# Attention weights exponentiated key by key without subtracting the row maximum, and normalised after the value matmul

## The chip, the cores and the metric

One core of one Trainium2 chip. The metric is the device time of one execution in microseconds (us); less is better. Of the kernel before there are two unprofiled runs, 6692.37 and 6696.81 us (median 6694.59), and one profiled execution.

## What is computed

The reference is one layer on x of shape [2, 256, 128, 128] (batch, time, band, channel), all in float32. Three residual steps follow one another:

```python
xt = _ln(x, ln_t_w, ln_t_b).transpose(0, 2, 1, 3)
x = x + _mha(xt, t_wi, t_bi, t_wo, t_bo, H_T, cm).transpose(0, 2, 1, 3)
xf = _ln(x, ln_f_w, ln_f_b)
x = x + _mha(xf, f_wi, f_bi, f_wo, f_bo, H_F, bm)
xn = _ln(x, ln_n_w, ln_n_b)
h = jax.nn.gelu(xn @ w1.T + b1, approximate=False)
x = x + (h @ w2.T + b2)
```

`_mha` is attention with 4 heads of 32 channels: scores q.k / sqrt(32) plus a mask, softmax over the keys, the weighted sum of the values, and an output matrix. The first runs over the 256 times of each band under a causal mask (`cm`), the second over the 128 bands of each time under a mask that lets through keys at most 16 bands away (`bm`). The feed-forward widens 128 channels to 512. Matrices are normal numbers times 0.02, biases are zero, norm weights are one.

## The kernel before

The work is done in groups of four token tiles (`NT`) of 128 tokens by 128 channels.

**The time stage** has 128 groups of two bands each. `xt` is loaded for eight bands at once on SP's queue (L278), POOL adds the output bias into `rd` (L282), `attention` runs, and `rd` goes to a DRAM tensor `x1` (L287).

**The band stage** has 32 blocks of 16 time steps. A block loads `xb` (L299), adds the bias on POOL (L301), runs `attention` on four groups one after the other, and then the feed-forward on the same four (L310 to L332): `hp` (w1, L316), gelu on ACT (L317), `zp` (w2, L327), the sum on DVE (L331), and the store.

**Inside a group.** `norm_transposed` takes means and variances on DVE (L118, L119), the inverse deviation on POOL (L121, L122) and the normed tokens `xh` on DVE (L126), and transposes them on PE into `xp`. ACT moves `xp` to SBUF with the norm's weight and bias (`xnT`, L131). From there PE makes `qp`, `kp` and `vp` (L144, L148, L153); ACT writes `qT` and `kT` (L146, L150), DVE writes `v` (L157). A score bank `sp` holds two heads, with queries on the partitions and keys along the row. The mask is put in first by a bfloat16 matmul of the identity with a mask tile (L166), then come the score matmuls over the 32 channels of a head (L173). DVE takes the negated row maximum `nmax` (L181 for bands, L187 for time), ACT exponentiates with it as the bias and adds up each row (L195, one instruction per head and query tile, with its accumulator read). DVE takes the reciprocal (L203), POOL multiplies the weights (L206 or L214), PE transposes each 128x128 block of weights (`tp`, L221), DVE and ACT bring them back to SBUF as `pT` (L226, L228), and PE multiplies them with the values (`op`, L239). ACT copies `op` out (`oT`, L245), PE applies the output matrix (`yp`, L248), DVE adds it to the residual (L249).

The order of each engine's queue is set when the program is built, by the tile framework's scheduler. `ps` has four banks of PSUM for everything but the scores, `ps_s` two tiles of two banks. A manual dependency (L255) makes exponentials and gelus take turns by the block, since they need different ACT tables.

## Time and profile before

| | us |
|---|---|
| median of the two runs | 6694.59 |
| span of the profiled execution, first to last instruction | 6687.7 |
| time stage, first to last `yp` on t_wo | 43.0 to 3075.2 |
| band stage, first to last `yp` on f_wo | 3095.0 to 6651.6 |
| PE busy | 4965.1 (74%) |
| ACT busy | 3223.4 (48%) |
| DVE busy | 2769.3 (41%) |
| POOL busy | 2263.4 (34%) |
| mean granted TensorE clock | 0.840 |

The profiled execution has no time of its own beside its span; the median of the runs is 6.9 us above that span. The shares are means over two stages. In the views of the trace a row gives the engine, the source line, the operation, what it writes `<-` what it reads, the shapes and a count. In the timeline a row begins with its start and its length in us, and ends with the idle time before it and what ended that. PEld is the loading of weights into the array, which overlaps the matmuls. A float32 matmul stands in the trace as two passes, so four matmuls of 128 columns are counted as x8. In the table of windows the column PEclk is the granted TensorE clock, 1.00 or 0.50 at any moment.

### The profile page before, as it was taken

To read this page: it belongs to the slowest core of one execution; us is meant where nothing else is said; L and a number is where in the kernel's file an instruction comes from. 1 tells how busy PE (TensorE), PEld (TensorE's weight loads), DVE (VectorE), ACT (ScalarE), POOL (GpSimd) and SP (SyncE) were. 2 spreads that over 40 slices of the span, in tenths; PEclk is the share of its full clock that TensorE was granted. 3 is DMA by queue.
4 is the path that set the end of the run, shared out by engine and by line. 5 is a ranking of instruction groups with operands and counts; after the bars stand their busy time and mean duration, and the time that the engine had idled before them with its cause. 6 is when DMAs were issued, how large, how long until landed. Compare 5 with 4: busy or idle time off the path is not lost. (4 is left out here: it accounts for less than half of the span.)

```text
span 6687.7 us, 95401 instructions
## 1 busy us (share of the span) xinstructions
PE 4965.1 (74%) x34688; PEld 3392.3 (51%) x34816; DVE 2769.3 (41%) x8068; ACT 3223.4 (48%) x10688; POOL 2263.4 (34%) x2348
## 2 busy tenths in 40 slices
PE   6777777777777777777777777777676767677767
PEld 4444454444444444454555555555454545455555
DVE  4444444444444444434344444444344444444433
ACT  4444444444444444444454444444444444454544
POOL 4333333333333333433232323233333333233332
PEclk8878787778787877788888888888888888888888
DMA  1000000000000000000000000000000000000000
GB/s 48 20 24 25 23 20 24 24 23 20 24 24 23 20 24 23 24 20 20 24 15 24 14 26 14 26 13 26 13 26 13 26 13 26 13 26 13 20 7 13
DMA packets 222968, 141.61 MB, mean 21 GB/s; under 512 B 7968, under 2 KB 205984, under 8 KB 222496
## 3 DMA queue, kind: packets, MB, share of 16 engines
q1 hardware_dynamic: 221248, 134.45, 7.1%
q8 instruction: 274, 4.49, 0.3%
q14 instruction: 198, 1.62, 0.1%
q10 hardware_dynamic: 1248, 1.05, 0.1%
HBM read 68.36 MB, written 67.11 MB: 20 GB/s over the span
## 5 line engine op out<-in xcount | busy, mean ns | idle before, releaser
L195 ACT ACTIVATE p<-sp,nmax 128x128 f32<-128x128 f32 (+1 forms) x4096 | 1547.6, 414 | 870.0 <-DVE nmax L187 553.6
L221 PE MATMUL tp<-ident,p 128*128 128x128 f32 x5120 | 1207.6, 401 | 275.6 <-POOL p L206 228.0
L221 PEld LDWEIGHTS tp<-ident,p 128*128 128x128 f32 x5120 | 930.1, 209 | 743.0 <-POOL p L206 394.6
L214 POOL TENSOR_TENSOR p<-p,rsum 128x256 f32<-128x256 f32 (+1 forms) x1024 | 823.9, 826 | 952.2 <-DVE rsum L203 820.9
L206 POOL TENSOR_TENSOR p<-p,rsum 128x1024 f32<-128x1024 f32 x256 | 485.2, 1895 | 1493.5 <-DVE rsum L203 1493.5
L195 ACT ACTIVATION_READ_ACCUMULATOR p<-sp,nmax 128x1 f32 x4096 | 929.0, 227 | 0.0
L228 ACT COPY pT<-tp 128x384 f32<-128x384 f32 (+1 forms) x768 | 395.1, 518 | 945.8 <-PE tp L221 942.5
L226 DVE COPY pT<-tp 128x384 f32<-128x384 f32 (+1 forms) x768 | 453.8, 598 | 698.9 <-PE tp L221 689.3
L173 PE MATMUL sp<-kT,qT 32*128 32x128 f32 (+1 forms) x8192 | 740.7, 362 | 0.0
L166 PEld LDWEIGHTS <-ident_b 128*128 128x128 bf16 x1536 | 193.8, 128 | 1007.0 <-issue 663.8
L166 PE MATMUL sp<-mask_t,ident_b 128*128 128x384 bf16 x1024 | 383.1, 472 | 384.6 <-ACT p L195 381.7
L203 DVE RECIPROCAL rsum<-rsum 128x4 f32<-128x4 f32 (+1 forms) x768 | 141.9, 185 | 1221.9 <-ACT p L195 1204.0
L239 PE MATMUL op<-pT,v 128*32 128x128 f32 (+1 forms) x8192 | 526.6, 319 | 86.6 <-DVE pT L226 55.0
L166 PE MATMUL sp<-mask_f,ident_b 128*128 128x512 bf16 x384 | 204.3, 601 | 517.0 <-ACT p L195 517.0
L173 PEld LDWEIGHTS sp<-kT,qT 32*128 32x128 f32 x8192 | 490.8, 214 | 172.9 <-issue 142.1
L317 ACT ACTIVATE hT<-hp,cols_sb 128x512 f32<-128x512 f32 x512 | 351.8, 687 | 392.3 <-PE hp L316 389.5
L187 DVE TENSOR_REDUCE nmax<-sp 128x2 f32<-128x256 f32 (+1 forms) x1024 | 505.0, 545 | 56.6 <-PE sp L173 56.5
L131 ACT ACTIVATE xnT<-xp,cols_sb 128x512 f32<-128x512 f32 x384 | 298.4, 777 | 475.0 <-PE xp L129 475.0
L327 PEld LDWEIGHTS zp<-w2T_sb,hT 128*128 128x128 f32 x4096 | 487.5, 192 | 61.5 <-issue 58.4
L316 PE MATMUL hp<-xnT,w1T_sb 128*128 128x512 f32 x1024 | 471.9, 599 | 42.8 <-ACT xnT L131 27.8
L327 PE MATMUL zp<-w2T_sb,hT 128*128 128x128 f32 x4096 | 499.0, 275 | 0.1
L121 POOL TENSOR_SCALAR rstd<-mv 128x4 f32<-128x4 f32 x384 | 91.8, 242 | 1190.5 <-DVE mv L119 1190.5
(55 smaller groups left out, 5974.5 us busy)
## 6 DMA issues: line engine op xcount, KB each, us to landing
xt<-in_x SPq DMA_DIRECT2D x64, 512.0 KB, 5.5
x<-rd SPq DMA_DIRECT2D x256, 128.0 KB, 1.9
out<-res SPq DMA_DIRECT2D x128, 256.0 KB, 2.3
xb<-x SPq DMA_DIRECT2D x32, 0.5 KB, 6.2
w1T_sb<-in_w1T ACTq DMA_DIRECT2D x1, 256.0 KB, 5.4
w2T_sb<-in_w2T ACTq DMA_DIRECT2D x1, 256.0 KB, 7.1
t_wiT_sb<-in_t_wiT ACTq DMA_DIRECT2D x1, 192.0 KB, 2.5
f_wiT_sb<-in_f_wiT ACTq DMA_DIRECT2D x1, 192.0 KB, 4.5
```

What stands on the lines that cost most here:

```text
L166: nc.tensor.matmul(sp[:, j, 0 : nb * P], ident_b, mask.rearrange("p a b -> p (a b)"), start=True, stop=False,)
L173: nc.tensor.matmul(sp[:, j, n * P : (n + len(ks)) * P], qT[r, qi * P : (qi + 1) * P], kT[r, ks[0] * P : (ks[-1] + 1) * P], start=False, st ...
L187: nc.vector.tensor_reduce(nmax[:, :, ri : ri + 1], sp[:, :, n * P : (n + len(ks)) * P], AX.X, ALU.max, negate=True,)
L195: e = nc.scalar.activation(p[:, j, n * P : (n + len(ks)) * P], sp[:, j, n * P : (n + len(ks)) * P], AF.Exp, bias=nmax[:, j, ri : ri + 1], ...
L206: nc.gpsimd.tensor_tensor(pv, pv, rsum.rearrange("p j n -> p (j n)").unsqueeze(2).to_broadcast([P, 2 * nb, P]), ALU.mult,)
L214: nc.gpsimd.tensor_tensor(pv, pv, rsum[:, :, ri : ri + 1].to_broadcast([P, 2, len(ks) * P]), ALU.mult,)
L221: nc.tensor.transpose(tp[:, n * P : (n + 1) * P], p[:, j, n * P : (n + 1) * P], ident)
L226: nc.vector.tensor_copy(t, tp[:, 0 : nb * P])
L228: nc.scalar.copy(t, tp[:, 0 : nb * P])
L239: nc.tensor.matmul(op[r, qi * P : (qi + m) * P], v[:, ki, r], pT[bi, h][:, n * P : (n + m) * P], start=first, stop=last,)
L316: nc.tensor.matmul(hp_, w1T_sb[:, j * P : (j + 1) * P], xnT, start=True, stop=True)
L327: nc.tensor.matmul(zp[:, i], hT[:, j, i * P : (i + 1) * P], w2T_sb[:, j, :], start=(j == 0), stop=(j == NI - 1),)
```

## The change

- `fold` (new, runs once at the start) multiplies the norm's weights and the scale into copies of the projection matrices (`wf`, `w1f`), carries the norm's biases into `bq` and into the row that is added to the residual, and negates the output matrices (`wn`). It bounds the scores by the Gram matrices of the folded query and key weights and leaves a flag, which every engine loads into a register.
- If the flag is set, `bounded_path` runs, otherwise `shifted_path`, which is the code of before. Both are in the program. The bound is a property of the weights. For these weights the sum that is tested is about 128 times 0.0016 times 0.051, that is 0.0105, and the limit is 900/(128 x 129), that is 0.0545, so the flag is set.
- In `bounded_path` a score bank holds one head with the keys on the partitions and the queries along the row. There is no mask matmul, no maximum, no bias of the exponential and no accumulator. One exponential covers 384 columns (time, L539) or 512 (bands, L582).
- Masked weights are set to 0 afterwards, in SBUF, by POOL's affine_select: four of 512 elements per partition per time group (L542), two of 2048 per band group (L584).
- The weights are already in the layout that the value matmul reads, so the transposes `tp` and the copies `pT` are gone, and so are the reciprocal and POOL's multiplication.
- A matmul of the weights with a matrix of ones gives the sum over keys, repeated over a head's 32 channels (`rp`, L561 and L565, or L596). `finish` takes the inverse on ACT as exp(-ln(rp)), sharpens it with a Newton step and scales `op` on DVE (t, u, oT, L508 to L512), and then comes `yp` with the negated matrix.
- `xnT` is a plain copy on ACT; `kT` is a copy on DVE instead of an ACT instruction.
- PSUM is one ring of eight banks.
- A table set that has both exp and ln is loaded ahead of each run of exponentials (L630).
- Groups are still written one after the other.

```diff
--- before.py
+++ after.py
...
+def fold(tc, k):
...
+            wf = const.tile([P, 3 * C], F32, name=f"wf{a}")
+            nc.vector.tensor_scalar(wf[:, 0:C], wi[:, 0:C], col(c0), scale, ALU.mult, ALU.mult)
+            nc.vector.tensor_scalar(wf[:, C : 3 * C], wi[:, C : 3 * C], col(c0), None, ALU.mult)
+            wn = const.tile([P, C], F32, name=f"wn{a}")
+            nc.vector.tensor_scalar(wn, wo, -1.0, None, ALU.mult)
...
+            for h in range(H):
+                r = slice(h * D, (h + 1) * D)
+                nc.vector.tensor_reduce(tests[r, 3 * a : 3 * a + 1], gs[r, r], AX.X, ALU.add)
...
+        tp = pp.tile([P, 6], F32, name="tp")
+        nc.tensor.matmul(tp, k.ones, tests, start=True, stop=True)
+        ok = fp.tile([P, 6], F32, name="ok")
+        for a in range(2):
+            nc.vector.tensor_scalar(
+                ok[:, 3 * a : 3 * a + 1], tp[:, 3 * a : 3 * a + 1], SAFE * SAFE / (C * (C + 1)), None, ALU.is_le
+            )
+            nc.vector.tensor_scalar(
+                ok[:, 3 * a + 1 : 3 * a + 3], tp[:, 3 * a + 1 : 3 * a + 3], LARGE, None, ALU.is_le
...
+        allok = fp.tile([P, 1], F32, name="allok")
+        nc.vector.tensor_reduce(allok, ok, AX.X, ALU.min)
+        flag = const.tile([P, 1], I32, name="flag")
+        nc.vector.tensor_copy(flag, allok)
+    return nc.values_load(flag[0:1, 0:1], min_val=0, max_val=1)
...
+            xnT = work.tile([P, NT * P], F32, name="xnT")
+            nc.scalar.copy(xnT, xp)
+            return xnT
...
+            qp = bank([P, NT * P], "qp")
+            nc.tensor.matmul(qp, wf[:, 0:C], xnT, start=True, stop=True)
+            qT = work.tile([P, NT * P], F32, name="qT")
+            nc.scalar.activation(qT, qp, AF.Identity, bias=k.bq[a], scale=1.0)
...
+            nc.tensor.matmul(kp, wf[:, C : 2 * C], xnT, start=True, stop=True)
+            kT = work.tile([P, NT * P], F32, name="kT")
+            nc.vector.tensor_copy(kT, kp)
...
+            v = work.tile([P, NT, C], F32, name="v")
+            nc.vector.tensor_copy(v, vp)
+            return qT, kT, v
...
+        def exp(p, sp, first):
+            e = nc.scalar.activation(p, sp, AF.Exp)
+            after(e, first)
+            last_exp[0] = e.ins
...
+        def finish(op, rp, dst, a, first):
...
+            ln = work.tile([P, NT * P], F32, name="ln")
+            e = nc.scalar.activation(ln, rp, AF.Ln)
+            after(e, first)
+            r0 = work.tile([P, NT * P], F32, name="r0")
+            exp_ins = nc.scalar.activation(r0, ln, AF.Exp, scale=-1.0)
+            after(exp_ins, first)
+            last_exp[0] = exp_ins.ins
+            t = work.tile([P, NT * P], F32, name="t")
+            nc.vector.tensor_tensor(t, rp, r0, ALU.mult)
+            u = work.tile([P, NT * P], F32, name="u")
+            nc.vector.tensor_tensor(u, op, r0, ALU.mult)
+            oT = work.tile([P, NT * P], F32, name="oT")
+            nc.vector.scalar_tensor_tensor(oT, t, 2.0, u, ALU.subtract, ALU.mult)
+            yp = bank([P, NT, C], "yp")
+            for i in range(NT):
+                nc.tensor.matmul(yp[:, i], oT[:, i * P : (i + 1) * P], k.wn[a], start=True, stop=True)
+            nc.vector.tensor_tensor(dst, yp, dst, ALU.add)
...
+        def over_time(src, dst, first):
...
+            xnT = norm_transposed(src)
+            qT, kT, v = project(xnT, 0)
+            W = 3 * P
+            p = work.tile([P, S, H, W], F32, name="pt", bufs=2)
+            for s in range(S):
+                a = 2 * s * P
+                for h in range(H):
+                    r = rows_of(h)
+                    sp = bank([P, W], "sp")
+                    nc.tensor.matmul(
+                        sp[:, 0 : 2 * P], kT[r, a : a + P], qT[r, a : a + 2 * P], start=True, stop=True
+                    )
+                    nc.tensor.matmul(
+                        sp[:, 2 * P : W], kT[r, a + P : a + 2 * P], qT[r, a + P : a + 2 * P],
+                        start=True, stop=True,
+                    )
+                    exp(p[:, s, h, :], sp, first)
+                for n in (0, 2):
+                    blk = p[:, s, :, n * P : (n + 1) * P]
+                    nc.gpsimd.affine_select(
+                        out=blk, in_=blk, compare_op=ALU.is_ge, fill=0.0, base=0,
+                        pattern=[[0, H], [1, P]], channel_multiplier=-1,
+                    )
+            op = bank([P, S, 2 * P], "op")
+            for s in range(S):
+                for h in range(H):
+                    r = rows_of(h)
+                    nc.tensor.matmul(
+                        op[r, s, :], v[:, 2 * s, r], p[:, s, h, 0 : 2 * P], start=True, stop=False
+                    )
+                for h in range(H):
+                    r = rows_of(h)
+                    nc.tensor.matmul(
+                        op[r, s, P : 2 * P], v[:, 2 * s + 1, r], p[:, s, h, 2 * P : W],
+                        start=False, stop=True,
+                    )
+            rp = bank([P, S, 2 * P], "rp")
+            for h in range(H):
+                nc.tensor.matmul(
+                    rp[rows_of(h), :, :], k.ones[:, 0:D], p[:, :, h, 0 : 2 * P], start=True, stop=False
+                )
+            for h in range(H):
+                nc.tensor.matmul(
+                    rp[rows_of(h), :, P : 2 * P], k.ones[:, 0:D], p[:, :, h, 2 * P : W],
+                    start=False, stop=True,
+                )
+            finish(op.rearrange("p s q -> p (s q)"), rp.rearrange("p s q -> p (s q)"), dst, 0, first)
...
+        def over_bands(src, dst, first):
...
+            xnT = norm_transposed(src)
+            qT, kT, v = project(xnT, 1)
+            p = work.tile([P, H, NT, P], F32, name="pf", bufs=2)
+            for h in range(H):
+                r = rows_of(h)
+                sp = bank([P, NT * P], "sp")
+                for i in range(NT):
+                    c = slice(i * P, (i + 1) * P)
+                    nc.tensor.matmul(sp[:, c], kT[r, c], qT[r, c], start=True, stop=True)
+                exp(p[:, h].rearrange("p i q -> p (i q)"), sp, first)
+            for s in (1, -1):
+                nc.gpsimd.affine_select(
+                    out=p, in_=p, compare_op=ALU.is_ge, fill=0.0, base=BAND,
+                    pattern=[[0, H], [0, NT], [-s, P]], channel_multiplier=s,
+                )
+            op = bank([P, NT * P], "op")
+            for i in range(NT):
+                c = slice(i * P, (i + 1) * P)
+                for h in range(H):
+                    r = rows_of(h)
+                    nc.tensor.matmul(op[r, c], v[:, i, r], p[:, h, i, :], start=True, stop=True)
+            rp = bank([P, NT * P], "rp")
+            for h in range(H):
+                nc.tensor.matmul(
+                    rp[rows_of(h), :], k.ones[:, 0:D], p[:, h].rearrange("p i q -> p (i q)"),
+                    start=True, stop=True,
+                )
+            finish(op, rp, dst, 1, first)
...
+        def exp_tables():
+            e = nc.scalar.preload_act_table_set(EXP_SET)
+            after(e, last_gelu[0])
+            return e.ins
+        first = exp_tables()
...
+    k = load_constants(ctx, tc, x, t_wiT, t_woT, f_wiT, f_woT, w1T, w2T, cols, rows)
+    bounded = fold(tc, k)
+    with tc.If(bounded > 0) as cmp:
+        bounded_path(tc, k, x, out)
+    with cmp.Else():
+        shifted_path(tc, k, x, out)
```

The feed-forward is as before, with `w1f` and the folded bias `b1`. The names below are those of the tables above; a number behind a name is a buffer's.

What PE issues at a border between two time groups, before (the last of a group's transposes and masks, the value matmuls, the output matrix, and the next group's transposes of its tokens):

```order
L221 MATMUL tp<-ident,p 128x128 x6
L166 LDWEIGHTS ident_b
L166 MATMUL sp<-mask_t,ident_b 128x384
...
L221 MATMUL tp<-ident,p 128x128 x2
L239 MATMUL op<-pT,v 32x256 x4
L239 MATMUL op<-pT,v 32x128 x4
...
L248 MATMUL yp<-t_woT_sb,oT 128x128 x4
L129 MATMUL xp<-ident,xh 128x128 x4
L144 MATMUL qp<-xnT,t_wiT_sb 128x512
```

and with the change:

```order
L535 MATMUL sp<-qT,kT 128x128
L550 MATMUL op<-pt,v 32x256 x4
L555 MATMUL op<-pt,v 32x128 x4
...
L561 MATMUL rp<-pt,ones 32x512 x4
...
L565 MATMUL rp<-pt,ones 32x2x128 x4
L515 MATMUL yp<-wn_106,oT 128x128 x4
L466 MATMUL xp<-ident,xh 128x128 x4
L474 MATMUL qp<-xnT,wf_103 128x512
```

Between the scores and `op` stand no matmuls any more, and between `rp` and `yp` none either. The next group's first matmul, `xp`, stands behind `yp` as before.

The same for a band group, before:

```order
L173 MATMUL sp<-kT,qT 128x128 x16
L166 LDWEIGHTS ident_b
L166 MATMUL sp<-mask_f,ident_b 128x512
...
L221 MATMUL tp<-ident,p 128x128 x8
...
L239 MATMUL op<-pT,v 32x128 x16
L248 MATMUL yp<-f_woT_sb,oT 128x128 x4
```

and with the change:

```order
L484 MATMUL vp<-wf_143,xnT 128x128 x4
L581 MATMUL sp<-qT,kT 128x128 x16
L593 MATMUL op<-pf,v 32x128 x16
L596 MATMUL rp<-pf,ones 32x512 x4
L515 MATMUL yp<-wn_146,oT 128x128 x4
```

The two runs of eight transposes that stood between scores and values are gone, and a run of four matmuls of 512 columns is new.

What DVE issues at a border between two band groups, before (the residual of one group, the statistics and normed tokens that its feed-forward will need, and the next group's values):

```order
L249 TENSOR_TENSOR x_26550<-yp,x_26550 128x512
L118 BN_STATS stats<-x_26550 128x6 x4
L119 BN_AGGR mv<-stats 128x2 x4
L126 TENSOR_SCALAR xh<-x_26550,mv,rstd 128x128 x4
L157 COPY v<-vp 128x512
```

and with the change:

```order
L516 TENSOR_TENSOR x_16068<-yp,x_16068 128x512
L455 BN_STATS stats<-x_16068 128x6 x4
L456 BN_AGGR mv<-stats 128x2 x4
L463 TENSOR_SCALAR xh<-x_16068,mv,rstd 128x128 x4
L481 COPY kT<-kp 128x512
L488 COPY v<-vp 128x512
```

The copy `kT`, which the scores wait for, now stands behind `xh`, and `xh` waits for POOL's rstd.

686 lines of the change are left out of this document (433 added, 253 removed).

## The prediction, as it was made before the result

> **What bounds the kernel now.** I read the page first, then the groups of instructions, the timeline of one group of each stage, and last the windows with the granted clock.
>
> ```profile
> span 6687.7 us, 95401 instructions
> PE 4965.1 (74%) x34688; PEld 3392.3 (51%) x34816; DVE 2769.3 (41%) x8068; ACT 3223.4 (48%) x10688; POOL 2263.4 (34%) x2348
> ```
>
> No engine is full, so a chain of waits sets the time. A time group from one `yp` to the next:
>
> ```profile
> 2002.77 1.16 PE L248 MATMUL yp<-t_woT_sb,oT 128*128 128x128 f32 x8 [0.78 <-ACT oT L245]
> 2003.76 0.60 PE L129 MATMUL xp<-ident,xh 128*128 128x128 f32 x4
> 2004.40 0.78 ACT L131 ACTIVATE xnT<-xp,cols_sb 128x512 f32<-128x512 f32 x1 [1.69 <-PE xp L129]
> 2005.23 1.12 PE L144 MATMUL qp<-xnT,t_wiT_sb 128*128 128x512 f32 x2 [0.87 <-ACT xnT L131]
> 2008.03 0.95 PE L173 MATMUL sp<-kT,qT 32*128 32x128 f32 x16
> 2010.50 0.47 ACT L195 ACTIVATE p<-sp,nmax 128x256 f32<-128x256 f32 x1
> 2010.95 0.36 ACT L195 ACTIVATE p<-sp,nmax 128x128 f32<-128x128 f32 x1
> 2012.28 3.22 POOL L214 TENSOR_TENSOR p<-p,rsum 128x256 f32<-128x256 f32 x4 [3.52 <-DVE rsum L203]
> 2024.37 1.03 PE L239 MATMUL op<-pT,v 128*32 128x256 f32 x12 [0.43 <-DVE pT L226]
> 2025.43 0.69 ACT L245 ACTIVATE oT<-op,cols_sb 128x512 f32<-128x512 f32 x1 [0.93 <-PE op L239]
> 2026.17 1.16 PE L248 MATMUL yp<-t_woT_sb,oT 128*128 128x128 f32 x8 [0.78 <-ACT oT L245]
> ```
>
> The next group's `xp` is issued only behind `yp`, so the period of 23.40 us (2002.77 to 2026.17) is the length of the chain. `yp` to scores takes 5.26, scores to `yp` 18.1. A band group, and the feed-forward of a block:
>
> ```profile
> 4017.92 1.16 PE L248 MATMUL yp<-f_woT_sb,oT 128*128 128x128 f32 x8 [0.78 <-ACT oT L245]
> 4023.19 1.72 PE L173 MATMUL sp<-kT,qT 32*128 32x128 f32 x32
> 4025.71 0.37 ACT L195 ACTIVATE p<-sp,nmax 128x128 f32<-128x128 f32 x1 [2.62 <-DVE nmax L181]
> 4036.43 1.06 PE L239 MATMUL op<-pT,v 128*32 128x128 f32 x26 [0.38 <-ACT pT L228]
> 4038.27 1.16 PE L248 MATMUL yp<-f_woT_sb,oT 128*128 128x128 f32 x8 [0.78 <-ACT oT L245]
> 4058.62 1.16 PE L248 MATMUL yp<-f_woT_sb,oT 128*128 128x128 f32 x8 [0.78 <-ACT oT L245]
> 4091.61 1.02 PE L144 MATMUL qp<-xnT,f_wiT_sb 128*128 128x512 f32 x2
> ```
>
> The period is 20.35 us; the last `yp` of a block to the next block's `qp` takes 33.0. The stages end here:
>
> ```profile
> L248 PE MATMUL yp<-t_woT_sb,oT x1024: 275/275/377, 43.0 to 3075.2; 128*128 128x128 f32 x171
> L248 PE MATMUL yp<-f_woT_sb,oT x1024: 275/275/582, 3095.0 to 6651.6; 128*128 128x128 f32 x171
> ```
>
> A time group takes (3075.2 - 43.0)/127 = 23.9 us on the mean, a block of bands (6687.7 - 3079)/32 = 112.8.
>
> The last thing to read is PE's clock (the column behind POOL's).
>
> ```profile
> 43.00:3075.00 3032.00, 2341.70 (x15245) 1497.72 (x15247) 1279.34 (x3762) 1437.18 (x5080) 1136.09 (x1387) 0.80 0.08 23
> 3079.00:6687.70 3608.70, 2600.47 (x19315) 1880.73 (x19441) 1464.08 (x4176) 1771.89 (x5565) 1101.99 (x918) 0.87 0.06 19
> 2004.64:2008.05 3.41, 2.82 (x14) 1.75 (x14) 1.41 (x9) 1.91 (x3) 1.79 (x3) 1.00 0.26 77
> 2008.05:2011.47 3.42, 0.93 (x17) 0.63 (x17) 2.64 (x5) 1.33 (x7) 0.71 (x1) 1.00 0.00 0
> 2014.88:2018.29 3.41, 3.41 (x17) 2.17 (x15) 1.47 (x4) 1.75 (x9) 1.30 (x3) 0.50 0.00 0
> 2018.29:2021.71 3.42, 3.42 (x16) 2.87 (x15) 1.84 (x5) 2.74 (x11) 1.83 (x3) 0.50 0.00 0
> 2021.71:2025.12 3.41, 2.98 (x38) 1.72 (x38) 0.56 (x1) 0.65 (x2) 0.71 (x1) 1.00 0.00 0
> 4004.85:4008.27 3.42, 0.00 (x0) 0.10 (x1) 1.67 (x2) 2.79 (x17) 0.00 (x0) 1.00 0.00 0
> 4008.27:4011.68 3.41, 1.55 (x6) 1.08 (x7) 0.41 (x2) 2.90 (x18) 2.02 (x2) 0.50 0.00 0
> ```
>
> The clock changes at steps of 3.41 us. It halves after a step in which PE did little (0.93 busy, or nothing) and comes back after a step that was full (2018.29). Step 2014.88 was full too and brought nothing; half of its work is `sp`, which uses 32 of 128 rows, so I count such passes at a quarter. Every stretch of PE work below therefore has two prices.
>
> **The change part by part.** The other rows that carry prices:
>
> ```profile
> L228 ACT COPY pT<-tp 128x512 f32<-128x512 f32 x256 | 149.8, 585 | 468.2 <-PE tp L221 468.2
> L249 DVE TENSOR_TENSOR x<-yp,x 128x512 f32<-128x512 f32 x128 | 88.5, 691 | 482.3 <-PE yp L248 482.3
> L97 POOL TENSOR_SCALAR_AFFINE_SELECT mask_f<-mask_f 128x512 bf16<-128x512 bf16 x2 | 1.3, 634 | 0.1
> masks.py:199 POOL TENSOR_SCALAR_AFFINE_SELECT ident<-ident 128x128 f32<-128x128 f32 x1 | 0.3, 292 | 0.0
> L301 POOL TENSOR_TENSOR x<-xb,rows_sb 128x2048 f32<-128x2048 f32 x32 | 145.6, 4550 | 4.8 <-DMA xb<-x 2.4
> ```
>
> *A time group at the full clock.* (a) `yp` to `qp`: 2.46 now, 2.27 with the copy at 585 ns. (b) `qp` to scores 2.80, unchanged: DVE's copy of `kT` (0.69) replaces ACT's 0.69. (c) The first head's scores are two passes of 384 columns at 0.11 us per 128, 0.66, and 0.2 until the reader starts: 0.86. Before, nmax stood here and the first exponential started 2.1 after `sp`. (d) Eight exponentials of 384 columns instead of sixteen with accumulator reads. An ACTIVATE of 256 columns and its read repeat after 0.45 (2010.50 to 2010.95), so I take 0.47 for 384 without a read: 3.8 with the tail. (e) The mask: the row of 128 float32 elements has the same 292 ns as bfloat16, and 634 - 292 for 384 more gives 0.89 ns each, so 512 cost 0.63. The first half's two selects run under the later exponentials; of the second half's, one lies on the path, 0.83 with handovers. (f) `op` of the second half and `rp`. Matmuls of 32 columns run four at a time (26 passes of 128 in 1.06), so 0.11 buys four: 2 x 384 columns of `op` and 2 x 768 of `rp` for each of four heads, 1.94. (g) ln 0.69, exp 0.69 (the `oT` row), t 0.62 and u 0.69 (L249), oT 0.65, with 0.5 of handovers: 3.8. Sum 16.3.
>
> Removed from the path: nmax, reciprocal, POOL's products, 24 transposes, the copies `pT`, eight mask matmuls. DVE's stats, POOL's rstd and `rd`, and SP's stores are issued at the same places and lie under the exponentials as before.
>
> *The same at the half clock.* `yp` and `xp` cost 1.34 more, the projections 2.6, the first scores 0.66, (f) 1.94: 22.8.
>
> *Which of the two.* During (g) PE has nothing to do for 3.8 us, longer than a step, so the clock has halved when `yp` starts. At that clock `yp` and `xp` take 2.7, then comes a gap of 0.8, then 5.2 of projections and the scores. The first step that is at least three quarters full ends between 6 and 10 us after `yp`, about 8, when the projections are nearly through: 1.34 + (8 - 3.5)/2 = 3.6 lost. Then the clock lasts, since the selects' pause is broken by the first half's `op`. I take 16.3 + 3.3 = 19.6 us (3.3, because (f) sometimes and the projections not always pay), 4.3 less than 23.9: 128 x 4.3 = 550 us gained, bounds 140 (22.8) and 970 (16.3).
>
> *A band group at the full clock.* (a) 2.27; (b) 2.80, where `xh` now stands ahead of `kT` on DVE and waits for POOL's rstd, which costs up to 1.5 when the projections are fast and nothing when they are slow; (c) eight passes of 128 on the first head, 0.89 + 0.2; (d) four exponentials of 512, 0.57 apart, 2.4; (e) two selects of 2048 elements, 292 + 1920 x 0.89 = 2.0 each. They cover all heads, so both follow the last exponential, and `op` is queued behind them: 4.15. (f) `op` 0.88 and `rp` 0.86; (g) 3.8. Sum 18.2. Here PE is idle for 5 to 6 us ahead of (f), so (f) runs at the half clock, +1.75; its 3.5 us are too short to bring the clock back; then (g) halves again, and the start of the group loses 3.6 as above. Sum 23.6, against 20.35 before. The first group of a block starts at the full clock behind the feed-forward, `qp` to `yp` 17.8. The feed-forward starts at the half clock now: 33.0 + 1.3 + about 2.1 = 36.4. Block: 17.8 + 3 x 23.6 + 36.4 = 125.0, with two waits for stores and table loads left where they were. That is 12.2 more than 112.8: 32 x 12.2 = 390 us lost. Bounds: -150 (full clock, 108) and +530 (129.5).
>
> *`fold` and the branch*: some twenty short steps of PE and DVE with a handover each, and the loads of x start behind them; 10 to 50 us, I take 25. The program holds both paths, but the one not taken isn't executed.
>
> Sum: 6687.7 - 550 + 390 + 25 = 6553. My terms leave out semaphore waits of a few tens of ns at some forty places of a group, for which I add 0.15 us per group, 40: 6593 for the span. The median of the runs is 6.9 above the span: **6600 us**.
>
> **Rivals.**
>
> *The clock falls only after a step without any PE work.* Then a time group's pause of 3.8 us would hit a whole step of 3.41 one time in nine and the group stay near 16.8, and band groups near 22: 128 x 16.8 + 32 x (17.0 + 3 x 22 + 35) + 60 = 5990 us. The row at 2008.05 speaks against it: 0.93 busy, and half the clock behind it. The Trainium skill ("TensorE: Matmul & The Clock Gate", Part 1) describes it so: half rate is the default, a busy window of 3.4 us releases it and an idle one brings it back; this trace has the length of the window and the two rates, but falls after partly busy ones. By that rule the result would be faster.
>
> *Time groups catch the clock earlier* than 8 us after `yp`, because steps lock to the groups' period: 17.5 to 18.5 per group, 6320 to 6450 us. For it: the bound on the left, 16.3, has PE idle ahead of `op` for under 3 us. Against: the pause (g) is longer than a step in every group.
>
> *Slower: the selects run at POOL's two-operand rate.* 4550 ns for 2048 (L301) instead of 2.0 adds 5.1 per band group and 0.64 per time group: 6600 + 650 + 80 = 7330 us. It decides from about 3.0 us per select of 2048 (6600 + 256 x 1.0 = 6860). Against it: the one float32 row stands at 292.
>
> *Slower: the half clock throughout*, since 32-row score matmuls don't bring it back: 128 x 22.8 + 32 x 129.5 + 80 = 7140 us. For it: 2014.88. Against it: the projections alone hold more than a step.
>
> *The flag is not set* and the old code runs: 6720 us.
>
> **How the numbers follow.** Forecast (6450 to 6800) 0.50; earlier clock 0.17; falls only when idle 0.07; slow selects 0.08; the half clock for longer than forecast, up to throughout (6800 to 7140), 0.16; flag 0.02. A measurement here can tell about 2% from no change, that is 6561 and 6828. Of the forecast 0.17 lies below 6561, so faster 0.17 + 0.17 + 0.07 = 0.41; same 0.33, the flag's 0.02 and 0.02 of the half clock = 0.37; slower 0.14 + 0.08 = 0.22. The range leaves out the fall-only-when-idle case below, and above the slow selects and 0.05 of the half clock: 6290 to 7000.
>
> **What would show it.** Right: `yp` to `yp` near 19.6 in the time stage and 23.6 in the band stage, the time stage shorter by 550 and the band stage longer by 390; PEclk at most 0.80 in both, 0.50 around every band `op`; selects at 0.63 and 2.0 us; no `tp`. Wrong: band groups under 20 us, selects above 3 us, or PEclk near 1.00 in the time stage.

## The result, and the profile after

The changed kernel takes 6321.72 us (two runs, 6314.48 and 6328.95) against 6694.59: ratio 0.9441, 95% interval 0.9423 to 0.9459, 5.6% faster. The forecast was 6600, 1.4% faster. The profiled execution has a span of 6327.0 us.

The page's head, as shown of before:

```profile
span 6327.0 us, 77114 instructions
PE 4254.3 (67%) x31270; PEld 2916.5 (46%) x31270; DVE 2110.8 (33%) x6318; ACT 1834.1 (29%) x3264; POOL 1777.9 (28%) x1830
```

All engines have less to do, and still none is full. The stages, cut at the last `yp` of the time stage (the clock is the column behind POOL's):

```profile
51.10:2386.00 2334.90, 1472.59 (x13221) 968.24 (x13222) 799.10 (x2243) 720.81 (x1525) 628.19 (x879) 0.84 0.11 30
2386.00:6327.00 3941.00, 2758.81 (x17916) 1933.43 (x17914) 1283.46 (x3920) 1106.34 (x1726) 1130.73 (x918) 0.71 0.06 17
```

The time stage went from 3032 to 2335 us. The band stage went from 3609 to 3941, although PE, VectorE and ScalarE issue fewer instructions there (PE 17916 for 19315) and VectorE and ScalarE are busy for less. PE is busy for longer with fewer matmuls, 2759 us for 2600, at a mean clock of 0.71 for 0.87; POOL's 1131 us stand for 1102. A time group in the timeline:

```profile
2000.14 2.05 PE L515 MATMUL yp<-wn,oT 128*128 128x128 f32 x8 [3.52 <-DVE oT L512]
2001.98 1.06 PE L466 MATMUL xp<-ident,xh 128*128 128x128 f32 x4
2003.71 1.12 PE L474 MATMUL qp<-xnT,wf 128*128 128x512 f32 x2 [0.68 <-ACT xnT L468]
2006.57 0.74 PE L532 MATMUL sp<-qT,kT 32*128 32x256 f32 x8
2007.56 3.17 ACT L492 ACTIVATE pt<-sp 128x384 f32<-128x384 f32 x8 [1.99 <-PE sp L535]
2011.48 0.64 PE L550 MATMUL op<-pt,v 128*32 128x256 f32 x8 [0.50 <-POOL pt L542]
2013.75 0.60 ACT L500 ACTIVATE ln<-rp 128x512 f32<-128x512 f32 x1 [3.02 <-PE rp L565]
2017.20 2.05 PE L515 MATMUL yp<-wn,oT 128*128 128x128 f32 x8 [3.57 <-DVE oT L512]
```

17.06 us from `yp` to `yp`, where 19.6 was forecast. `yp` (2.05) runs at half clock, `qp` (1.12) at full clock again. The clock's steps of the same stretch:

```profile
1999.82:2003.24 3.42, 2.90 (x12) 2.53 (x12) 1.03 (x3) 0.17 (x1) 0.00 (x0) 0.50 0.00 0
2003.24:2006.65 3.41, 2.94 (x16) 1.83 (x16) 2.05 (x10) 1.11 (x2) 1.41 (x2) 1.00 0.27 77
2006.65:2010.06 3.41, 1.74 (x36) 1.55 (x40) 0.67 (x1) 2.50 (x7) 1.86 (x4) 1.00 0.00 0
2010.06:2013.48 3.42, 2.92 (x48) 1.10 (x48) 0.00 (x0) 0.67 (x2) 1.67 (x3) 1.00 0.00 0
2013.48:2016.89 3.41, 0.15 (x4) 0.00 (x0) 1.81 (x3) 1.23 (x2) 0.00 (x0) 1.00 0.00 0
2016.89:2020.30 3.41, 2.90 (x12) 2.53 (x12) 1.02 (x3) 0.16 (x1) 0.00 (x0) 0.50 0.02 5
```

`yp` and `xp` together are busy for 2.90 us of one step of 3.42 at half clock, and the clock is back right behind it. A band group:

```profile
4025.74 2.08 PE L515 MATMUL yp<-wn,oT 128*128 128x128 f32 x8 [3.43 <-DVE oT L512]
4029.34 2.08 PE L474 MATMUL qp<-xnT,wf 128*128 128x512 f32 x2 [0.68 <-ACT xnT L468]
4034.50 2.82 PE L581 MATMUL sp<-qT,kT 32*128 32x128 f32 x32
4035.75 2.20 ACT L492 ACTIVATE pf<-sp 128x512 f32<-128x512 f32 x4 [3.61 <-PE sp L581]
4038.03 4.09 POOL L584 TENSOR_SCALAR_AFFINE_SELECT pf<-pf 128x2048 f32<-128x2048 f32 x2 [6.82 <-ACT pf L492]
4042.17 1.94 PE L593 MATMUL op<-pf,v 128*32 128x128 f32 x32 [4.85 <-POOL pf L584]
4045.88 0.60 ACT L500 ACTIVATE ln<-rp 128x512 f32<-128x512 f32 x1 [7.93 <-PE rp L596]
4049.24 2.08 PE L515 MATMUL yp<-wn,oT 128*128 128x128 f32 x8 [3.43 <-DVE oT L512]
```

23.50 us, as forecast (23.6): PE waits 4.85 for the selects, and `op` and the next `yp` and `qp` run at half clock. Here `yp` straddles two steps:

```profile
4023.93:4027.34 3.41, 1.60 (x7) 1.61 (x8) 1.72 (x3) 0.00 (x0) 0.00 (x0) 0.50 0.00 0
4027.34:4030.75 3.41, 2.73 (x9) 1.76 (x8) 1.84 (x9) 0.59 (x1) 2.04 (x3) 0.50 0.00 0
4030.75:4034.17 3.42, 3.42 (x9) 1.92 (x8) 1.81 (x5) 0.69 (x1) 0.46 (x1) 0.50 0.00 0
4034.17:4037.58 3.41, 3.15 (x36) 2.84 (x34) 0.69 (x1) 1.83 (x4) 0.00 (x0) 1.00 0.00 0
```

Neither the step with 1.60 us of work nor the one with 2.73 brings the clock back; that takes until 8.4 us after the start of `yp`.

One wait grew, and that was not forecast. At a change of tile of x (a tile is loaded for four groups):

```profile
2023.82 1.00 SPq L641 DMA_DIRECT2D xt<-in_x  x2
2028.28 1.06 DVE L455 BATCH_NORM_STATS2 stats<-xt 128x6 f32<-128x128 f32 x5 [4.79 <-DMA xt<-in_x]
2029.26 0.67 DVE L488 COPY v<-vp 128x512 f32<-128x512 f32 x1
2030.08 0.69 PE L550 MATMUL op<-pt,v 128*32 128x256 f32 x8 [4.00 <-DVE v L488]
```

The statistics of a later group wait for their tile, the copy `v` is queued behind them, and PE waits 4.00 us for `v`. That group takes 20.6 to 21.4 us and often the next one 19.8. In the kernel before the statistics waited for their tile as well (us in total, times, longest):

```profile
DVE stats L118 <- DMA xt<-in_x: 70.2, 31, 6.8
```

There the group in which they waited, one in four, took some 26.2 us and the next one 22.3.

### The profile page after: what moved, and what is told of

Read it like the earlier page. It is cut to its first block, busy times and chain, and to the rows that moved or that the text cites. A ratio compares the mean times of both kernels' runs of the same rounds, so it can differ in the third digit from the quotient of the medians.

```text
span 6327.0 us, 77114 instructions
## 1 busy us (share of the span) xinstructions
PE 4254.3 (67%) x31270; PEld 2916.5 (46%) x31270; DVE 2110.8 (33%) x6318; ACT 1834.1 (29%) x3264; POOL 1777.9 (28%) x1830
## 4 chain that ended last, share of the span: by engine, by line
PE 57%; ACT 16%; POOL 11%; DVE 10%; DMA 3%; issue 2%; SPq 0%; ACTq 0%; POOLq 0%; DVEq 0%
PE hp L608 8%; PE yp L515 8%; POOL pf L584 8%; PE zp L619 7%; ACT pt L492 5%; PE qp L474 5%; ACT pf L492 4%; PE op L593 4%; PE kp L479 4%; PE vp L484 4%; PE xp L466 4%; PE rp L596 4%; DVE oT L512 3%; DVE t L508 3%; ACT r L503 3%; DVE u L510 2%
## 5 line engine op out<-in xcount | busy, mean ns | idle before, releaser
L515 PE MATMUL yp<-wn,oT 128*128 128x128 f32 x2048 | 526.6, 439 | 892.8 <-DVE oT L512 892.8
L515 PEld LDWEIGHTS yp<-wn,oT 128*128 128x128 f32 x2048 | 455.0, 327 | 1172.1 <-DVE oT L512 661.3
L508 DVE TENSOR_TENSOR t<-rp,r 128x512 f32<-128x512 f32 x256 | 177.1, 692 | 2392.9 <-ACT r L503 2392.9
L584 POOL TENSOR_SCALAR_AFFINE_SELECT pf<-pf 128x2048 f32<-128x2048 f32 x256 | 515.1, 2012 | 1245.8 <-ACT pf L492 1237.0
L608 PE MATMUL hp<-xnT,w1f 128*128 128x512 f32 x1024 | 548.9, 687 | 21.6 <-ACT xnT L468 21.6
L609 ACT ACTIVATE hT<-hp,b 128x512 f32<-128x512 f32 x512 | 352.0, 688 | 496.0 <-PE hp L608 496.0
L492 ACT ACTIVATE pt<-sp 128x384 f32<-128x384 f32 x1024 | 405.9, 518 | 300.4 <-PE sp L535 300.4
L474 PE MATMUL qp<-xnT,wf 128*128 128x512 f32 x512 | 373.4, 819 | 152.1 <-ACT xnT L468 152.1
L484 PEld LDWEIGHTS vp<-wf,xnT 128*128 128x128 f32 x2048 | 344.2, 238 | 173.8 <-issue 142.3
L542 POOL TENSOR_SCALAR_AFFINE_SELECT pt<-pt 128x512 f32<-128x512 f32 x512 | 314.7, 634 | 318.9 <-ACT pt L492 318.9
L459 POOL TENSOR_TENSOR rstd<-rstd,mhalf 128x4 f32<-128x4 f32 x384 | 398.9, 1041 | 16.1
L581 PE MATMUL sp<-qT,kT 32*128 32x128 f32 x4096 | 359.0, 282 | 27.6 <-DVE kT L481 27.6
```

Source lines behind the costliest of these rows:

```text
L459: nc.gpsimd.tensor_tensor(rstd, rstd, k.mhalf, ALU.pow)
L474: nc.tensor.matmul(qp, wf[:, 0:C], xnT, start=True, stop=True)
L484: nc.tensor.matmul(vp[:, i], xnT[:, i * P : (i + 1) * P], wf[:, 2 * C : 3 * C], start=True, stop=True)
L492: e = nc.scalar.activation(p, sp, AF.Exp)
L508: nc.vector.tensor_tensor(t, rp, r0, ALU.mult)
L515: nc.tensor.matmul(yp[:, i], oT[:, i * P : (i + 1) * P], k.wn[a], start=True, stop=True)
```

## The experiments

**Theory**: the halves of the change act apart; group lengths are set by where PE's pauses and work fall in the clock's steps; the long time groups come from the statistics ahead of `v`. **Rivals**: the chains on ACT, POOL and DVE alone set the lengths; or one stage's loss is made by the other. The runs of a kernel agree within 0.6%; times are medians of four.

**The two halves apart.** The band stage of before behind the new time stage:

```diff
-        for b in range(B):
-            x1v = k.x1[b].rearrange("t f c -> f t c")
...
+    shifted_path(tc, k, x, out, bands_only=True)
```

> The time stage of the changed kernel with the band stage of the kernel before. Theory: the two halves of the change do not touch each other, the band half costs 3941 - 3612 = 329 us, so the time is 6327 - 329 = 5998 us, within 20. Rival: part of what the band stage seems to lose is handed to it by the time stage (a clock or buffers left in another state), and then the band stage of before takes more than 3612 us here and the time is above 6050.

5980.21 us. That is 18 us below the 5998 expected and within the 20 allowed, so the halves add: the time half alone is worth 715 us (6695.53 in that comparison), the band half costs 341.

**A time group's chain made longer.** Two kernels, of which the first was meant as the other's base: the load of x written one tile earlier, and then also

```diff
             nc.vector.tensor_tensor(u, op, r0, ALU.mult)
+            if a == 0:
+                nc.vector.tensor_tensor(u, op, r0, ALU.mult)
```

> The load of the next tile of x is issued a whole tile (four groups) earlier in the time stage, nothing else is moved. Theory: in the changed kernel every fourth time group is long because VectorE's BN_STATS wait for that load and the copy of v stands behind them; the wait is some 4 us, and the clock that falls in it costs about 2.8 us more in that group and the next. 31 tiles by 6.5 us is 200 us: 6327 falls to about 6120, every time group takes 17.07 us (128 by 17.07 is 2185 us of time stage against 2335), and TensorE's idle time before the value matmuls no longer names v. Rival: the long groups come from the change of tile in another way (stores of rd, the buffer of xt), and then at most the first wait goes: 6290 or more. A second rival: without the stall, the groups find another length than 17.07 us, since nothing sets them back into step with the clock every fourth time; then the stage is 128 times that length.

6326.41 us where 6120 was expected: no change. The scheduler places the loads of x by when a buffer comes free, and SP's queue reads the same as without the edit. So this tells nothing of the wait, and only gives the base for the next.

> With the load of x a tile ahead, as in the run before, VectorE's product u is computed twice in each time group (0.69 us more in the chain between the sums and the output projection). Theory (the groups lock to the clock's steps of 3.41 us): the group cannot become 17.07 + 0.69; it goes to six steps, 20.48 us, or changes between five and six, and the time stage is 250 to 435 us longer than in the run with the load ahead alone. Rival (no lock, 17.07 is only the length of the chain): each group is 0.69 us longer, 88 us in all, and the groups have 17.76 us.

6642.87 us, 316 more for 88 us of work. The groups:

```profile
1979.11 2.04 PE L517 MATMUL yp<-wn,oT 128*128 128x128 f32 x8 [4.30 <-DVE oT L514]
1999.57 2.05 PE L517 MATMUL yp<-wn,oT 128*128 128x128 f32 x8 [4.25 <-DVE oT L514]
```

and its steps:

```profile
1978.16:1981.57 3.41, 2.46 (x11) 2.49 (x12) 1.09 (x3) 0.00 (x0) 0.00 (x0) 0.50 0.00 0
1981.57:1984.99 3.42, 2.75 (x6) 1.21 (x5) 1.87 (x9) 0.78 (x2) 0.74 (x2) 0.50 0.26 77
1984.99:1988.40 3.41, 3.41 (x14) 2.24 (x16) 0.88 (x2) 0.49 (x1) 1.73 (x2) 0.50 0.00 0
```

20.46 us, six steps, as the theory had it. `yp` starts 0.95 into its step, the step stays at 2.46 us busy, and the clock comes back two steps later, behind the projections: what the prediction had assumed for 19.6. The rival (17.76) is out.

**Work in PE's pause of a time group.** Two matmuls with the identity, overwritten by `yp` (such matmuls are called the fill); the same with `u` twice. Three forms: the scheduler free, the order of `xp` behind `yp` held by a dependency, and the fill also held behind the last `rp`:

```diff
             yp = bank([P, NT, C], "yp")
+            for _ in range(2):
+                e = nc.tensor.matmul(yp.rearrange("p i c -> p (i c)"), k.ident, xnT, start=True, stop=True)
+                after(e, last_rp[0])           # third form
...
-                nc.tensor.transpose(xp[:, i * P : (i + 1) * P], xh[:, i, :], k.ident)
+                e = nc.tensor.transpose(xp[:, i * P : (i + 1) * P], xh[:, i, :], k.ident)
+                after(e, last_yp[0])           # second and third form
```

> In the time groups alone, two 128x512 matmuls with the identity, overwritten by the output projection, stand on TensorE between the sums and the output projection; the bands are the changed kernel's. Theory: the gap between the sums and the output projection is the only place where a time group loses its clock; with it filled the groups go from 17.07 to the 16.3 us of the forecast's full clock, no group slips, and only the wait of some 4 us for the next tile of x stays, every fourth group: 128 by 16.3 and 31 by 4 is 2210 us of time stage against 2335, and the time 6327 - 125 = 6200 us (6170 to 6240). Rival: the added matmuls (2 by 0.86 us at full clock, 1.7 each at half) come in the way of the output projection and the group stays at 17 us or more: 6320 to 6420.

> The fill in the time groups, as in the run before, and VectorE's product u computed twice (0.69 us more in each group's chain), which cost 316 us without the fill (6643 against 6326). Theory (a group's length jumps in steps because the clock falls): with the clock held, the same 0.69 us costs 0.69 us a group, 88 us (60 to 110) over the run with the fill alone. Rival (the jump has another cause, such as a buffer or a queue that the late product holds back): 250 us or more over it, again.

5916.16 and 5886.11 us, both far below what either theory gave. The program's order had changed with the fill: `xp`, the projections and most scores of the next group now stood ahead of `yp`. Half of the groups took some 13 us (12.94 to 12.97 without the second `u`), the others mostly 14 to 20; the means are 15.2 and 14.9. The pair tests order and clock at once, and decides nothing on the clock.

> The fill of the time groups once more (two 128x512 matmuls between the sums and the output projection), with the order of the changed kernel held: the transposes of the next group stand behind the output projection of this one, which the earlier run with this fill (5916 us) had turned round. Theory: 5916 us came from two things, the clock and the order; the clock alone takes the groups from 17.03 to 16.3 us and removes the long groups that follow a fall of the clock, while the wait for x stays: 128 by 16.3 and 31 by 4 is 2210 us against 2335, the time 6200 us (6160 to 6240). Rival: the clock was all of it, and the time is 5916 again. Second rival: the order was all of it, 6300 to 6340.

> The run before it (fill in the time groups, order held) with VectorE's product u computed twice, 0.69 us more in each group's chain. Theory (without the fill this cost 316 us because the clock then came back a step later): with the clock held it costs its own length, 0.69 us by 128 is 88 us (60 to 110) over the run before. Rival: the jump from five steps to six has another cause than the clock, and it is 250 us or more over the run before.

6579.83 and 6649.18 us. The first is none of the times named; the second is 69 us above it, inside the 60 to 110 expected, but not for the reason given. The fill had moved ahead of the last sums:

```profile
1514.05 1.04 PE L565 MATMUL rp<-pt,ones 128*32 128x512 f32 x8
1515.02 1.98 PE L516 MATMUL yp<-xnT,ident 128*128 128x512 f32 x4
1517.17 0.61 PE L569 MATMUL rp<-pt,ones 128*32 128x256 f32 x8
1517.86 0.60 ACT L501 ACTIVATE ln<-rp 128x512 f32<-128x512 f32 x1 [5.02 <-PE rp L569]
1521.22 1.48 PE L518 MATMUL yp<-wn,oT 128*128 128x128 f32 x8 [3.43 <-DVE oT L513]
```

So it stood on the path, the pause of 3.43 stayed, and the clock still fell. The groups took 20.58 us; with the second `u` they alternated between 19.73 and 21.31, 20.52 on the mean. The first has a pair of 19.0 and 17.7 every tenth group or so, the second single groups of 22.6 instead, which makes the 69 us.

> Two 128x512 matmuls in the time groups behind the last matmul of the sums and ahead of the output projection, the order of the changed kernel held for all else. Theory: the clock no longer falls in this gap, so a group has the full-clock chain, 16.3 us, and none slips; the wait for x stays (31 by 4 us): 2210 us of time stage against 2335, 6200 us in all (6160 to 6240). Rival: the clock had come back by the projections anyway and the two matmuls only delay the output projection: 6330 to 6450.

> The run before it with VectorE's product u computed twice in each time group, 0.69 us more in the chain. Theory (a group's length follows the clock's steps only while the clock falls): with the clock held it costs its own 0.69 us, 88 us in all (60 to 110) over the run before, where the same edit without a fill cost 316 us. Rival: 250 us or more over the run before.

6173.15 and 6215.37 us. The first is the time expected, for another reason. The groups did not become 16.3 but stayed at 17.07; what went were PE's wait for `v`, since the statistics now stood behind `v` in VectorE's queue, and the slips (pairs of longer groups such as 18.6 and 19.6, on which more below). The clock no longer falls ahead of `yp` and falls behind the scores instead:

```profile
1490.67:1494.08 3.41, 1.73 (x32) 0.83 (x27) 0.00 (x0) 3.15 (x8) 1.43 (x3) 1.00 0.62 160
1494.08:1497.50 3.42, 2.93 (x24) 1.14 (x28) 2.08 (x11) 0.00 (x0) 1.03 (x2) 0.50 0.54 154
```

With the second `u` the groups take 17.76 and 16.34 in turn, 17.05 on the mean:

```profile
1542.12 1.16 PE L521 MATMUL yp<-wn,oT 128*128 128x128 f32 x8 [2.24 <-DVE oT L515]
1559.88 1.16 PE L521 MATMUL yp<-wn,oT 128*128 128x128 f32 x8 [2.25 <-DVE oT L515]
1576.22 1.16 PE L521 MATMUL yp<-wn,oT 128*128 128x128 f32 x8 [2.24 <-DVE oT L515]
```

One group in two has a step at half clock, the other none. The stage cost 42 us more, outside the 60 to 110 expected. So 0.69 us more in each chain cost nothing where groups stood at five steps; the 42 us are groups of 21 us at some changes of tile, where PE waits for `v` again (46.4 us in all). "With the clock held" was never true here. What is shown is narrower: in these orders of PE's queue, in which the clock falls, most groups come to whole steps, five or six, alone or in pairs, to within 0.1 us. The group of 16.34 without a fall puts the chain at full clock, without the second `u`, at 15.65 us; two groups of the run without it did pass without a fall, and took 15.64 and 15.67.

**Work in PE's pauses of a band group.** Three matmuls with the identity ahead of `op`, two ahead of `yp`, first with the scheduler free, then with the order held:

```diff
             op = bank([P, NT * P], "op")
+            for _ in range(3):
+                nc.tensor.matmul(op, k.ident, xnT, start=True, stop=True)
```

> In the band groups alone, three 128x512 matmuls with the identity, whose result is overwritten, stand on TensorE between the score matmuls and the value matmuls, and two more between the sums and the output projection. Theory: the band groups of the changed kernel (22.1, 23.5 and 23.7 us) are long because the clock falls to half in those two gaps; with work in them it stays up, the groups fall to 18.2 to 19 us, the block from 122.9 to 105 to 108 us, and the time from 6327 to 5750 to 5850 us, though 32 by 4 by 5 more matmuls run. Rival: the groups are long by their chain on ScalarE, GpSimd and VectorE, which the clock does not touch: then the time stays at 6327 or rises by what the added matmuls stand in the way, up to 100 us.

> The fills of the band groups (three 128x512 matmuls between scores and value matmuls, two between sums and output projection) with the order of the changed kernel held. Theory: the clock accounts for most of the difference between 6327 and the 5526 us of the run that filled the bands without holding the order: groups 18.2 to 19 us instead of 22.1 to 23.7, block 105 to 108 us, time 5750 to 5850 us, and the order for the rest. Rival: the order (the next group's projections in the gap) was nearly all, and the time here is 6200 or more.

5526.19 free, where the next projections moved ahead of `yp`, and 5706.72 held; both lie below the 5750 to 5850 expected, the second by 43 us. It is the clean one:

```profile
4047.32 1.16 PE L518 MATMUL yp<-wn,oT 128*128 128x128 f32 x8 [1.54 <-DVE oT L513]
4055.16 2.84 PE L594 MATMUL op<-xnT,ident 128*128 128x512 f32 x6
4060.08 1.08 PE L599 MATMUL op<-pf,v 128*32 128x128 f32 x32 [2.08 <-POOL pf L588]
4065.45 1.16 PE L518 MATMUL yp<-wn,oT 128*128 128x128 f32 x8 [1.51 <-DVE oT L513]
```

and the whole band stage, with its clock:

```profile
2372.00:5699.00 3327.00, 2806.99 (x19151) 1817.18 (x19150) 1265.93 (x3918) 1102.66 (x1721) 1131.64 (x918) 0.97 0.07 20
```

18.13 us for most groups (some 19 to 19.6) and 104.0 a block: with the clock at 0.97 a band group has the forecast's full-clock sum, 18.2. So the half clock, and not the length of the selects, makes the band half slower than before, whose groups took 20.35; with 640 matmuls of 512 columns more, the time falls by 615 us. Both pauses were filled at once, so these runs do not tell what each costs.

**The wait for x.**

```diff
-        xpool = ctx.enter_context(tc.tile_pool(name="xpool", bufs=3))      # first
+        xpool = ctx.enter_context(tc.tile_pool(name="xpool", bufs=4))
-        small = ctx.enter_context(tc.tile_pool(name="small", bufs=6))      # second, alone
+        small = ctx.enter_context(tc.tile_pool(name="small", bufs=3))
```

> The pool of the tiles of x has four buffers instead of three, so that the load of a tile waits for a buffer that came free a tile earlier; the fills are not in it. Theory: the wait of VectorE's BN_STATS for x (136.9 us in the changed kernel) goes, and with it the long group at every change of tile and the fall of the clock that follows it: 31 by 6.5 us is 200 us, 6327 falls to about 6120. Rival: a long group follows each time the groups' start has crept over the clock's step (17.03 us against five steps of 3.41 us, 17.07), which the waits for x only bring earlier: then a long pair (18.6 and 19.6, some 4 us more) stays every 15 to 20 groups, and the time is 6150 to 6200. Third: the load was not what was late, and nothing changes, 6327.

> The pool of the small tiles (statistics, means, 1/sigma) has three buffers instead of six; nothing else is changed. The statistics of a group can then run three groups ahead at most, and those of the next tile of x no longer stand on VectorE, waiting for its load, ahead of the copy of v. Theory: BN_STATS' wait for x (136.9 us) and TensorE's wait for v (79.0 us) go, and with them the long groups of 20.6 to 21.3 us and the 19.8 that follow: 31 by 6.5 us is 200 us, 6327 falls to 6120 (6080 to 6180). Rival: as with the load written earlier (6326) and the fourth buffer (6306) the time does not fall below 6280, and the long groups have another cause.

6305.55 and 6214.00 us; the second lies between the 6080 to 6180 of its theory and the 6280 of its rival. With a fourth buffer the scheduler placed the statistics a tile earlier too, and they waited no less (159.0 us). With fewer buffers for the statistics they run less far ahead and the wait is gone; the first row is the changed kernel's, the second that of the run with fewer buffers:

```profile
L455 DVE BATCH_NORM_STATS2 stats<-xt 128x6 f32<-128x128 f32 x512 | 105.8, 279 | 136.9 <-DMA xt<-in_x 136.9
```

```profile
L455 DVE BATCH_NORM_STATS2 stats<-xt 128x6 f32<-128x128 f32 x512 | 111.3, 281 | 10.0 <-DMA xt<-in_x 5.9
```

The mean group falls from 18.35 to 17.47 us, 112 us in all and not 200: every 16 groups or so, a pair of 18.6 and 19.6 stays. Groups of 17.03 creep 0.04 a time against the steps until `yp` begins ahead of one; the waits for x had only brought that earlier. This is the first rival named for the run with four buffers.

**Order and clock together.** First the fills of both stages with four buffers; then, without fills, the next group's front ahead of `yp`; then that with the scores ahead of `yp` in the time stage, the fill ahead of the bands' `op`, and three buffers of statistics. In outline:

```diff
+        qkv = front(first group)
         for each group:
-            over_time(src, rd, first)
+            tail = over_time(qkv, rd, first)     # scores to oT
+            qkv = front(next group)              # xp, qp, kp, vp
+            tail()                               # yp and the residual
```

> The fills in the time groups and in the bands, and four buffers for the tiles of x. Theory: the three work on different waits and their gains add: 5526 us of the bands' fill alone, less 125 for the fill in the time groups, less 124 for the wait for x (31 by 4; the clock does not fall behind it any more): 5277 us, 5240 to 5320. Rival: the loads of x take the place of a wait that comes next (the copies on VectorE behind the statistics), and the time is 5380 to 5420.

> No fills: the next group's transposes and projections are written ahead of this group's output projection, in both stages, so that this work lies in the gap between the sums and the output projection. Theory: in the time groups TensorE's longest gap is then gone, the clock stays up and the groups take 13 to 14 us: 2335 falls to about 1900 us. In the bands the gap of some 5 us between scores and value matmuls stays and the clock still falls in it, so that a group takes 19 to 20.5 us instead of 23.6: 32 blocks by 3 groups by 3.5 us is 340 us less. Together 5550 us (5450 to 5700). Rival: with the gap between scores and values open, the bands lose nearly all again to half clock (groups 22 us or more): 5800 to 5900. Second rival: the clock alone makes the difference, and an order without fills brings less than 200 us.

> A version for the time: in the time stage the next group's transposes, projections and scores ahead of this group's output projection; in the bands transposes and projections ahead of it, as in the run without fills (5549 us), and three 128x512 matmuls between scores and value matmuls that hold the clock; three buffers of statistics. Theory: the time groups take 13 us each (12.94 where the fill had brought this order), 128 by 13 is 1670 us; the block of bands falls from 102.3 us to 92 to 96, 32 of them 2950 to 3070 us; 60 us for the start: 4680 to 4800 us. Rival: without the fill in the time groups the clock falls between scores and values and they take 15.5 us or more: 5000 us or more.

5094.85, 5548.64 and 4745.38 us. The first gained more than the sum expected, which had put the time fill at 125 us; with what the three runs alone had measured (796 for the bands' fill, 406 for the time fill with its turned order, 16 for the buffer) the sum is 5105. The second met its time by luck, with its parts wrong: time groups took 17.27 us on the mean and not 13 to 14, bands 15.9 to 16.9 and not 19 to 20.5 (block 102.4). The third is the fastest, ratio to before 0.7099 (0.7082 to 0.7116), in the 4680 to 4800 expected; most time groups took 11.89 us where 13 was expected, blocks 98.4 where 92 to 96 was expected. Its page, and the two stages with their clock:

```profile
PE 3977.2 (84%) x32038; PEld 2660.2 (56%) x32038; DVE 2411.1 (51%) x6318; ACT 1807.6 (38%) x3264; POOL 1822.4 (38%) x1830
```

```profile
50.00:1590.00 1540.00, 1284.36 (x13184) 846.97 (x13184) 755.44 (x2250) 705.40 (x1523) 680.56 (x883) 0.99 0.17 46
1590.00:4739.00 3149.00, 2665.64 (x18673) 1794.70 (x18672) 1626.23 (x3919) 1093.29 (x1725) 1124.82 (x918) 0.92 0.07 21
```

## Why the prediction was wrong in size

**The step that failed** is "Which of the two" in the time group: "The first step that is at least three quarters full ends between 6 and 10 us after `yp`", with 3.3 us lost. It ended 3.1 us after `yp` (2000.14 to 2003.24), since `yp` and `xp` at half clock last 2.9 us and fall inside one step. The loss was 1.3, `yp` to `qp` 3.57 against the full clock's 2.27, so this term was put 2.0 us a group too high, 256 us in all. The prediction had the durations for this (2.7 us at half clock) and did not ask how they lie in a step. In the bands, where `yp` straddles two steps, its sentence held: 8.4 us. The rival "time groups catch the clock earlier" (17.5 to 18.5 per group, 6320 to 6450) is what came true in its mechanism. Its numbers, met at 18.35 and 6321.72, were met by luck: the groups that only catch the clock earlier take 17.06, below its range, and the mean is lifted into it by a wait and slips that it did not have.

**The other terms of a time group.** (b) 2.86 for 2.80, (c) 0.99 for 0.86, (d) 3.17 for 3.8, (e) 0.75 for 0.83, (f) 2.27 for 1.94, (g) 3.45 for 3.8. Only (d) is off by much: eight exponentials repeat every 0.38 us and not 0.47. Together the chain is 17.06, 2.5 below the 19.6, of which 1.3 is half clock, so about 15.7 at full clock against the 16.3 of the sum; the groups without a fall gave 15.65.

**What was missed**: the wait of `v` behind the statistics, and the slips. They lift the mean from 17.06 to 18.35, 165 us; removing the wait gave 112. The trace of before had such a wait in it: the prediction took 23.40 for the group and 23.9 for the mean, and did not ask about the groups of 26.2 that make the difference. The prediction's sentence that DVE's stats "lie under the exponentials as before" holds only for groups inside a tile, and "as before" held a wait of 70.2 us. The time stage gained 128 x (23.88 - 18.35) = 708 us against 550.

**The bands were right**, part by part: (a) 3.60 for 3.61, (b) 5.16 for 5.06, (c) 1.25 for 1.09, (d) 2.20 for 2.4, (e) 4.22 for 4.15, (f) 3.71 for 3.49, (g) 3.36 for 3.8; selects of 2012 and 634 ns where 2.0 and 0.63 us were worked out from two rows. A block is 122.9 for 125.0, mainly since the first of its three periods from `yp` to `yp` caught the clock early too (22.1): 332 us lost (3941 for 3609) against 390. The start cost 8 us (first `yp` 51.1 for 43.0) against 25, and the allowance of 40 us for waits was not needed. One sign failed: the clock was to be at most 0.80 in both stages and was 0.84 in the time stage.

**The other rivals.** Selects at POOL's two-operand rate: 2012 ns, out. Half clock throughout: 0.84 and 0.71, out. The old path: no transposes of weights and no `pT` in the trace, out. "The clock falls only after a step without any PE work" gives 16.8 and 22 us for groups that were 17.06 and 23.5, and 5990 us in all; it is out by the step of 1490.67, in which PE was busy for 1.73 us and behind which the clock fell. That is the rule of the Trainium skill ("TensorE: Matmul & The Clock Gate", Part 1), which names an idle window; the trace differs here. The Trainium skill's free-running window of 3.4 us, in the same part, agrees with the steps, which keep their grid of 3.413 us from the first to the last.

## What to carry to other kernels

Where PE pauses between short bursts, lay its work on the grid of the clock's steps before pricing a term: the same burst brought the clock back in 3.1 us inside one step and in 8.4 across two, and the half clock behind the pauses of a band group turned that half of the change into a loss of 332 us. Idle matmuls in the pauses with the order held (149 us in the time groups, of which a part is the wait for `v`, and 615 in the bands, in two runs) and the next group's own matmuls there (773 in both stages) came to about the same, and both together took the kernel to 4745 us. After an edit read the order of the queues before the time: ten of the sixteen runs here fell outside the time expected of them, and in five of these (5526, 5916, 5886, 6580 and 5095 us) PE's queue had an order that the edit had not meant.

## What was unexpected in the hardware

A group whose chain is 15.65 us at full clock took 17.07, and 0.69 us more in the chain cost 3.4 us a group in one order (20.46) and nothing in two others (17.05 for 17.07, 20.52 for 20.58): with a clock that changes in steps, group lengths came to whole steps of 3.41 us, or near them. The blocks of bands show it best: 112.64 us on the median before and 122.88 with the change are 33 and 36 steps of 3.413, and 30 of the 31 periods from block to block in the changed kernel lie within 0.05 of a step of that. The band half lost three whole steps a block. With the clock at 0.97, in the run with the bands' pauses filled and the order held, none of the 31 does.

Busy time alone does not tell when the clock falls: behind 1.74 us (2006.65) it stayed, behind 1.73 (1490.67) it fell. The first step holds 1.63 us of scores, which use 32 rows, and 0.11 of `op`, which uses 32 columns; the second holds 0.70 and 1.02.

Work does tell. Give every 128 columns of a pass the 0.107 us that they take at the full clock (from `kp` to `vp`, two passes of 512, is 0.86), twice that at the half clock, and count a pass on 32 rows or 32 columns at a quarter. In the traces of the changed kernel and of the fifteen runs that keep its band stage, the full clock then stays behind a step with more than about 1.29 us of work, which is wrong for 295 of 16,995 steps; it comes back behind one with more than about 2.46, wrong for 156 of 10,876. With the passes on 32 rows counted in full, 2,022 and 292 are wrong. So the quarter that the prediction assumed for the scores comes out of these runs, and so, nearly, do its three quarters of a step: `yp` and `xp` are 2.58 us of work when they lie in one step, and the second step of the straddled `yp` (4027.34) holds 2.39. The two steps with which this began lie at the border, with 1.29 and 1.26.
